# A graph network on one core: output norms, R's sums and row sums moved within a hand-written order

## The chip, the core and the metric

The kernel runs on one core of a Trainium2 chip. The metric is the device time of one execution in microseconds, the median of three: 1462.17 us before the change (1462.06 to 1468.56). The profile is one further execution with the hardware profiler on: 1480.01 us, with a span of 1478.2 us. Engines are named as in the profile: PE (TensorE, matmuls), PEld (its weight loads), DVE (VectorE), ACT (ScalarE), POOL (GpSimd), SP (SyncE, which here only issues transfers).

## What is computed

Two graph layers on 2708 nodes with 256 features, in float32. Layer 0 is `x = layernorm(x + relu([x, adj @ x] @ W + b))`. Layer 1 makes, in two steps, an attention matrix A by nucleus ("top-p") selection, and a second product with the row-normalized adjacency R:

```python
R = S + eye(N);  R = R / R.sum(-1)
for n in range(2):
    probs = softmax(q(Xa) @ k(Xa).T)          # per row: keep the largest until 0.9 of the mass
    A = probs * mask;  A = A / A.sum(-1)      # row sums
    Xf = R @ Xf
    Xa = A @ Xa
    Z = Z + Xf @ U1[n].T + Xa @ U2[n].T
h = layernorm(X + Z) * g + b                  # "middle" norm
x = layernorm(x + h)                          # "end" norm
```

The kernel applies U1 and U2 before the products, so a product of A (or R) with a projected matrix gives an output directly. adj is sparse (0.3% and the diagonal): the rows that a block of R needs are gathered.

## The kernel before, in words

Rows are treated in 22 blocks of 128 (the last has 20). All engines run the order in which the instructions are written down; there is no scheduler. Each engine works through its own queue in that order and waits at semaphores, so a waiting instruction holds back everything behind it on the same engine.

There are four stages. Layer 0 fills the first 520 us or so. The first attention step and the lists of nonzero columns come next. The third stage, the loop at L1098 over `per`, runs from about 800 us to the end; the change lies there. It does the second attention step for all blocks, both products with R, and the output norms. The fourth is a short tail.

One turn of `per` is called a block here. It has six slots, `g` = 0 to 5 (L1109), and several row blocks are in flight in it:

- Row block `per` is on DVE: `finish2` (L950) finds its threshold and makes its mask. L959 multiplies below a bound (128x2720), L962 takes maxima of 20 segments, L559 and L561 put candidates in order, L972 to L987 find the threshold, L990 marks ties, L993 writes the masked weights and, as `tot`, their sum. L994 computes the same sum in another way, as z + mass - below (`kept`), and L996 takes its reciprocal `ra`.
- Row block `per - 1` is on PE: in each slot `turn` (L520) transposes four 128x128 pieces (L526), ACT copies them from PSUM (L529), and `products` (L535, L546) multiplies the pieces of the slot before with `ya`.
- Row blocks `per + 1` and `per + 2` are on ACT: trial levels (`try_act`, L905 and L908, 128x2708 each) and exponentials of logits (`exps2`, L801 and L805).
- R's product is cut into units of one matmul each (`r_units`, L701, L713), eight to a row block. Blocks 0 to 9 do the product of step 0, blocks 11 to 21 that of step 1 at 16 units each: 2, 3, 3, 2, 3, 3 by slot, so a row block of R begins in slots 0 and 3 and ends in slots 2 and 5. When one begins, its successor's rows are fetched into the other half of `yg` by seven indirect gathers that POOL issues (`y_load`, L677, L681), and its adjacency by SP (L687).
- A sum of R that has ended is taken by DVE one slot later: the list `later` holds it. `r_out` (L733) is L736 in step 0; in step 1 it calls `arrive` (L744, L751), which adds the part to a base kept in memory (`za_d`). The attention's part arrives likewise, in slot 1.
- When both parts have arrived, a row block is `ready`. `final_slot` (L1054) takes up to two of them in slot 3. In slot 4 it takes statistics of them and of the ones in their second norm (L1021, L1022, on DVE) and the root of the variances (L1064, on ACT). In slot 5 it does the reciprocal and a product (L1066, L1067, on DVE), the norms (L1031, on ACT), the store of finished blocks (L1052, issued by SP), and for new ones the scale and the addition on POOL (L1046, L1047).

`bulk` keeps figures per row block for one check at the end (`flags`); where a flag is set, another, general path computes everything anew. With this data it is not taken.

Of the kernel before, what the change touches and what calls it, by code (L numbers as in the profile page):

```python
# [9 lines left out]
FP = mybir.dt.float32  # L10
# [10 lines left out]
P = 128  # L21
# [7 lines left out]
WS = 5  # L29
# [119 lines left out]
def fast_path(ctx, tc, c, flags, fint, xT_d, x_d, w0_d, b0_d, w1_d, w2_d, w3_d, u1_d, u2_d, g_d, b_d):  # L149
# [521 lines left out]
    r_now = []  # L671
    r_in, a_in, y_in = {}, {}, {}
    arrived, loads, held = {}, {}, {}
    later = []
    ready = []

    def y_load(s, m):  # L677
# [23 lines left out]
    def r_units(n):  # L701
        for _ in range(n):
            s, m = r_queue[0]
            p = rows(m)
            if not r_now:
                r_now[:] = [ps_misc(), 0]
                if m + 1 < NB:
                    r_load(s, m + 1)
            acc, k = r_now
            a, y = r_in[s, m]  # L710
            kw = CW if k < CC else p
            rhs = v[:p, m, :] if s and k == CC else y[:kw, k, :]
            nc.tensor.matmul(acc[:p, :D], lhsT=a[:kw, k, :p], rhs=rhs, start=k == 0, stop=k == CC)  # L713
            r_now[1] += 1
            if k == CC:
                r_now.clear()
                r_queue.pop(0)
                r_in.pop((s, m))
                base = za_load(m) if s else None
                later.append(lambda s=s, m=m, acc=acc, base=base: r_out(s, m, acc, base))  # L720

    def za_load(m):

# [52 lines left out]

    bulk = small.tile([P, 4 + WS, NB], FP, tag="bulk", name="bulk", bufs=1)
    nc.gpsimd.memset(bulk[:, :3, :], 1.0)  # L780
    nc.gpsimd.memset(bulk[:, 3:, :], 0.0)

    class Block:

# [165 lines left out]
    def finish2(b):  # L950

        t, p = b.t, b.p
        sc = small.tile([P, 3 + 2 * WS], FP, tag="sc", name="sc", bufs=3)
        below, mass, nk = (sc[:p, i:i + 1] for i in range(3))
        num, run = bulk[:p, 4:, t], sc[:p, 3:3 + WS]
        need, kept, tot = (bulk[:p, i, t:t + 1] for i in range(1, 4))
        th = b.m
        e = e2(t)[:p]
        nc.vector.scalar_tensor_tensor(w[:p], e, b.d, e, op0=ALU.is_lt, op1=ALU.mult, accum_out=below)  # L959
        cand = small.tile([P, NS2 * 8], FP, tag="cand", name="cand", bufs=2)  # L960
        for i in range(NS2):
# [25 lines left out]
        nc.vector.tensor_scalar(part[:p], part[:p], th, None, op0=ALU.mult)  # L987
        W = NW // WS
        for i in range(WS):
            nc.vector.match_replace(w[:p, W * i:W * (i + 1)], part[:p, i, :], e[:, W * i:W * (i + 1)], 3.0e38)  # L990
            if i == WS // 2:
                yield
        nc.vector.scalar_tensor_tensor(e, w[:p], th, e, op0=ALU.is_gt, op1=ALU.mult, accum_out=tot)  # L993
        nc.vector.scalar_tensor_tensor(kept, mass, below, b.z, op0=ALU.subtract, op1=ALU.add)  # L994
        ra = small.tile([P, 1], FP, tag="ra", name="ra")
        nc.vector.reciprocal(ra[:p], kept)  # L996
        ras[t] = ra

    new, finals = [], []
    tail = []  # L1000

    mvs = small.tile([P, 4, 2], FP, tag="mvs", name="mvs", bufs=1)
# [4 lines left out]
    class Final:  # L1007
# [39 lines left out]
            nc.gpsimd.tensor_tensor(h[:p], h[:p], self.x1[:p], op=ALU.add)  # L1047

        def end(self):
            t, p = self.t, self.p  # L1050
            self.norm(self.h)
            nc.sync.dma_start(out=out_d[t * P:t * P + p, :], in_=self.h[:p])  # L1052

    def final_slot(i):  # L1054

        if i == 3:
            while ready and len(new) < 2:
                new.append(Final(*ready.pop(0)))
                new[-1].load()
        n = len(new) + len(finals)  # L1060
        if i == 4 and n:
            for k, f in enumerate(new + finals):
                f.stats(k)
            nc.scalar.activation(sds[:, :n], mvs[:, :n, 1], AF.Sqrt, bias=c.eps, scale=1.0)  # L1064
        if i == 5 and n:
            nc.vector.reciprocal(sds[:, :n], sds[:, :n])  # L1066
            nc.vector.scalar_tensor_tensor(nbs[:, :n], mvs[:, :n, 0], -1.0, sds[:, :n], op0=ALU.mult, op1=ALU.mult)  # L1067
            for f in finals:
                f.end()
            for f in new:  # L1070
                f.middle()
            finals[:] = new
            new.clear()

# [23 lines left out]
    for per in range(NB + 1):  # L1098
# [9 lines left out]
            b_exp = blocks[per + 2] = Block(per + 2)  # L1108
        for g in range(NG):  # L1109
            n = n_r * (g + 1) // NG - n_r * g // NG  # L1110
            now, later[:] = later[:], []
            if g == 0:
                if b_exp:
                    shift(b_exp, lg[0])
                r_units(n)
            if per:
                turn(t_mul, g, ya, accs[t_mul], e2(t_mul))
            if b_exp and g == 3:
                lg = logits(1, b_exp.t, 2)
            if g == NG - 1 and 3 < per + 3 < NB:  # L1120
                lg = logits(1, per + 3, 0)
            if g:
                r_units(n)
            if b_exp and g == 1:
                lg = logits(1, b_exp.t, 1)
            products(1 if per else 0)
            if b_exp and g in (0, 1, 3):
                exps2(b_exp, (g + 1) // 2, *lg)
            if b_act:
                for k, part in {0: ((0, 0),), 1: ((0, 1), (0, 2), (0, 3)), 2: ((1, 0),), 3: ((1, 1), (1, 2), (1, 3))}.get(g, ()):  # L1130
                    try_act(b_act, k, part)
            if g == 0:
                if b_dve:
                    last_level(b_dve)
                    masks = finish2(b_dve)
                    next(masks)
                if per > 1:

                    t = t_mul - 1
                    base = za_load(t)  # L1140
                    later.append(lambda t=t, base=base: arrive(t, base, accs.pop(t), ras.pop(t)[:rows(t)]))
            elif masks:
                next(masks, None)
                if b_exp and g == 5:
                    begin_search(b_exp)
            for f in now:
                f()
            if g:
                final_slot(g)
# [2 lines left out]

    nc.vector.tensor_scalar(flags[:, 2 * NB:3 * NB], bulk[:, 0, :], 1.0e30, None, op0=ALU.is_ge)
    nc.vector.tensor_scalar(flags[:, 3 * NB:4 * NB], bulk[:, 1, :], 0.0, None, op0=ALU.is_le)
    nc.vector.scalar_tensor_tensor(flags[:, 4 * NB:5 * NB], bulk[:, 2, :], 1.0 + TIE_EPS, bulk[:, 3, :],
                                   op0=ALU.mult, op1=ALU.is_lt)
    nc.vector.tensor_reduce(flags[:, 5 * NB:6 * NB], bulk[:, 4:, :].rearrange("p w t -> p t w"), AX.X, ALU.max)
    nc.vector.tensor_scalar(flags[:, 5 * NB:6 * NB], flags[:, 5 * NB:6 * NB], 8.0, None, op0=ALU.is_ge)
    nc.vector.tensor_reduce(fcol, flags, AX.X, ALU.add)
    products(0)  # L1160
# [3 lines left out]
    nc.vector.tensor_copy(fint, pf[:1, :1])  # L1164
    t = NB - 1
    base = za_load(t)
    while later:
        later.pop(0)()
    arrive(t, base, accs.pop(t), ras.pop(t)[:rows(t)])
    while ready or finals:  # L1170
        for g in (3, 4, 5):
            final_slot(g)
    assert not r_queue and len(arrived) == NB

# [359 lines left out]
```

## Time and profile before

| What | us | Where from |
|---|---|---|
| Timed, median of three | 1462.17 | times |
| Profiled span | 1478.2 | page |
| PE busy | 1302.5 (88%) | page, part 1 |
| DVE busy | 1047.2 (71%) | page, part 1 |
| ACT busy | 750.6 (51%) | page, part 1 |
| POOL busy | 624.6 (42%) | page, part 1 |
| One gather of step 1 (L681), mean | 0.967 | page, part 5 |
| L1046, mean | 1.645 | page, part 5 |

A line of the groups has the source line, the engine and the operation, what is written from what, the shape and the count; then busy time, the mean of one in ns, and the idle time of the engine ahead of it with what ended most of it. The list of waits gives, for pairs of waiting and waited-for instructions, the time in total, how often, and the longest. A line of the windows has the stretch, its length, the busy time and number of instructions of PE, PEld, DVE, ACT and POOL, then the clock granted to PE, the busy share of the transfer engines and their GB/s. A line of the timeline has the start, the duration, the engine, the source line, the operation, and in brackets how long the engine had been idle and what released it. "remote" and "another core or an unknown queue" stand where the profile found no releaser. In the changed kernel the lines from L995 on are shifted (L1046 becomes L1045).

### The profile page before, as it was taken

Reading aid. Unit: us, or ns where it says so; the run is one execution under the profiler, and the core shown is the slowest. Engines: PE = TensorE matmul, PEld = TensorE weight load, DVE = VectorE, ACT = ScalarE, POOL = GpSimd, SP = SyncE. Lnnn points to the kernel's source line nnn. Section 1 sums busy time; section 2 is a strip of 40 time slices with the busy share of each in tenths; the row PEclk is TensorE's granted clock in tenths of the full one; section 3 lists DMA queues with packets and bytes.
Section 4 is the critical chain, followed back from the end, with each engine's and each line's share of the span. In section 5 each row is a group of like instructions: output and inputs, shape, how many; then the busy total and the mean of one; then the engine's idle time right before and its main releaser. Section 6 shows DMA issues by size and latency. Waiting matters only on the chain.

```text
span 1478.2 us, 18958 instructions
## 1 busy us (share of the span) xinstructions
PE 1302.5 (88%) x5788; PEld 907.7 (61%) x5788; DVE 1047.2 (71%) x3500; ACT 750.6 (51%) x1351; POOL 624.6 (42%) x597
## 2 busy tenths in 40 slices
PE   8999999898999999999988599999878767787776
PEld 6877787534666666666654376767545555555553
DVE  2444546849788877677514699999987777777775
ACT  1000000145455555555544387878767777777741
POOL 1000000033644416765543667677154555555551
PEclk9999999999999999999997699999989889889996
DMA  6554444312221202322322454545142333333332
GB/s 179 179 164 150 150 149 150 107 55 77 71 70 61 63 9 73 95 66 65 64 85 84 137 164 130 171 132 163 49 140 84 103 107 108 107 116 122 108 112 52
DMA packets 92830, 157.94 MB, mean 107 GB/s; under 512 B 16356, under 2 KB 65196, under 8 KB 92720
## 3 DMA queue, kind: packets, MB, share of 16 engines
q1 hardware_dynamic: 66434, 100.59, 21.3%
q0 software_dynamic: 20544, 51.17, 13.1%
q10 hardware_dynamic: 5742, 4.89, 1.1%
q8 instruction: 48, 0.79, 0.2%
q14 instruction: 62, 0.51, 0.1%
HBM read 125.33 MB, written 31.26 MB: 106 GB/s over the span
## 4 chain that ended last, share of the span: by engine, by line
PE 55%; DVE 23%; ACT 12%; another core or an unknown queue 6%; issue 3%; DMA 0%; ACTq 0%; DVEq 0%
PE acc L546 17%; PE acc L255 14%; PE lg L506 6%; PE tr L526 4%; DVE cand L962 3%; PE misc L660 3%; DVE w L990 3%; DVE e L993 3%; DVE w L959 2%; ACT w L905 2%; ACT w L908 2%; PE acc L632 2%; ACT e L801 2%; DVE spare L561 2%
## 5 line engine op out<-in xcount | busy, mean ns | idle before, releaser
L546 PE MATMUL acc<-ya,wT 128*128 128x256 f32 (+1 forms) x924 | 247.6, 410 | 54.6 <-ACT wT L529 30.8
L529 ACT COPY wT<-tr 128x512 f32<-128x512 f32 (+2 forms) x264 | 134.2, 511 | 317.4 <-PE tr L526 145.3
L546 PEld LDWEIGHTS acc<-ya,wT 128*128 128x128 f32 (+1 forms) x924 | 180.6, 203 | 114.1 <-issue 48.6
L546 PE MATMUL acc<-x,wT 128*128 128x256 f32 (+1 forms) x924 | 234.4, 393 | 8.4 <-ACT wT L529 7.4
L681 POOL DMA_INDIRECT yg<-yf_d,ix x154 | 191.7, 1245 | 104.9 <-PE misc L713 46.1
L546 PEld LDWEIGHTS acc<-x,wT 128*128 128x128 f32 (+1 forms) x924 | 167.1, 192 | 90.9 <-issue 49.0
L713 PE MATMUL misc<-yg,adj_t 128*128 128x256 f32 (+1 forms) x660 | 181.7, 402 | 32.2 <-issue 20.4
L255 PE MATMUL acc<-y,adj_t 128*128 128x257 f32 (+1 forms) x924 | 208.8, 382 | 0.0
L365 POOL DMA_INDIRECT adj_t<-in_adj,ix x154 | 172.5, 1120 | 50.6 <-issue 39.6
L255 PEld LDWEIGHTS acc<-y,adj_t 128*128 128x128 f32 (+1 forms) x924 | 171.5, 189 | 34.0 <-issue 10.2
L681 POOL DMA_INDIRECT yg<-v_d,ix x154 | 148.9, 967 | 83.7 <-issue 40.4
L506 PE MATMUL lg<-k,q 64*128 64x512 f32 (+3 forms) x528 | 154.1, 611 | 25.4 <-ACT e L805 23.0
L526 PE MATMUL tr<-ident,e 128*128 128x128 f32 (+1 forms) x968 | 152.6, 277 | 22.7 <-issue 13.5
L713 PEld LDWEIGHTS misc<-yg,adj_t 128*128 128x128 f32 (+1 forms) x660 | 118.0, 193 | 85.3 <-issue 47.5
L526 PEld LDWEIGHTS tr<-ident,e 128*128 128x128 f32 (+1 forms) x968 | 117.3, 142 | 69.3 <-issue 42.5
L332 POOL DMA_DIRECT2D part_d<-e x1 | 0.6, 576 | 295.5 <-DVE e L331 295.5
L552 DVE MAX8 cand<-e 128x8 f32<-128x170 f32 (+1 forms) x352 | 88.2, 319 | 39.6 <-ACT e L513 23.0
L905 ACT ACTIVATE w<-e,st 128x2708 f32<-128x2708 f32 (+1 forms) x43 | 113.5, 2640 | 0.0
L908 ACT ACTIVATE w<-e,st 128x2708 f32<-128x2708 f32 (+1 forms) x42 | 111.0, 2642 | 0.1
L438 ACT COPY x1T<-tr 128x256 f32<-128x256 f32 (+1 forms) x22 | 8.0, 364 | 192.2 <-PE tr L437 192.2
L962 DVE MAX8 cand<-w 128x8 f32<-128x136 f32 (+1 forms) x440 | 94.4, 284 | 0.8
L1046 POOL TENSOR_TENSOR yg<-yg,gb 128x256 f32<-128x256 f32 x21 | 34.5, 1645 | 136.5 <-ACT yg L1031 136.5
(226 smaller groups left out, 1871.1 us busy)
## 6 DMA issues: line engine op xcount, KB each, us to landing
adj_t<-in_adj SPq DMA_DIRECT2D x44, 704.0 KB
adj_t<-adjc_d SPq DMA_DIRECT2D x44, 448.0 KB
adjc_d<-adj_t SPq DMA_DIRECT2D x22, 256.0 KB
base<-za_d SPq DMA_DIRECT2D x41, 128.0 KB
adjc_d<-adj_t SPq DMA_DIRECT2D x22, 192.0 KB
xt<-in_x ACTq DMA_DIRECT2D x21, 128.0 KB
x_d<-x SPq DMA_DIRECT2D x21, 128.0 KB
x1b_d<-xb SPq DMA_DIRECT2D x21, 128.0 KB
```

The source lines that it names most:

```text
L255: nc.tensor.matmul(acc[:p, :n], lhsT=halves[k // KH][:kw, k % KH, :p], rhs=y[:kw, k, :n], start=k == 0, stop=stop and k == NB - 1)
L365: nc.gpsimd.indirect_dma_start(out=a[:CW, i, :], out_offset=None, in_=adj_rows, in_offset=bass.IndirectOffsetOnAxis(ap=ix[:CW, m, i:i + 1] ...
L506: nc.tensor.matmul(lg[:p, h, :b - a], lhsT=q[o, t * P:t * P + p], rhs=keys[s][o, i, :b - a], start=True, stop=True)
L526: nc.tensor.transpose(tr[:kw, k % 4, :p], e[:p, k * P:k * P + kw], ident[:p, :p])
L529: nc.scalar.copy(wT[:, :full, :p], tr[:, :full, :p])
L546: nc.tensor.matmul(acc[:p, :D], lhsT=wT[:kw, k % 4, :p], rhs=y[:kw, k, :], start=k == 0, stop=k == NB - 1)
L552: nc.vector.max(dst[:p, i * 8:(i + 1) * 8], src[:p, i * step:i * step + w])
L681: nc.gpsimd.indirect_dma_start(out=y[:CW, i, :], out_offset=None, in_=rows_d, in_offset=bass.IndirectOffsetOnAxis(ap=ix[:CW, m, i:i + 1], ...
L713: nc.tensor.matmul(acc[:p, :D], lhsT=a[:kw, k, :p], rhs=rhs, start=k == 0, stop=k == CC)
L905: nc.scalar.activation(scr[:b.p, :N], e, AF.Relu, bias=b.nz, scale=b.l[k], accum_out=b.relu)
L908: nc.scalar.activation(scr[:b.p, :N], e, AF.Sign, bias=b.nz, scale=b.l[k], accum_out=b.sign)
L962: nc.vector.max(cand[:p, 8 * i:8 * i + 8], w[:p, SEG2 * i:SEG2 * (i + 1)])
```

## The change

It changes where in the order some instructions stand, and it takes one sum from another place:

- In `final_slot`, new blocks are taken in slot 2 and statistics made in slot 3. The root stands in slot 5, two slots behind its statistics. The reciprocal and the norms stand in slot 0 of the next block, behind `finish2`'s first part; the stores stand in slot 1, by the list `done`.
- `later` becomes two lists. A sum of R goes into the second one and is taken two slots behind its end; the attention's part still goes one slot on.
- The row sum `tot`, which L993 makes while it masks, is inverted directly. `below` and `mass` move into `bulk`, and the other form of the sum, which only the check needs, is formed once for all blocks at the end.

The purpose is to have an instruction wait for a result only when that result has had time to be made.

```diff
-    later = []
+    later = [[], []]
@@ r_units
-                later.append(lambda s=s, m=m, acc=acc, base=base: r_out(s, m, acc, base))
+                later[1].append(lambda s=s, m=m, acc=acc, base=base: r_out(s, m, acc, base))
@@ finish2
-        below, mass, nk = (sc[:p, i:i + 1] for i in range(3))
-        num, run = bulk[:p, 4:, t], sc[:p, 3:3 + WS]
-        need, kept, tot = (bulk[:p, i, t:t + 1] for i in range(1, 4))
+        num, run = bulk[:p, 5:, t], sc[:p, :WS]
+        need, below, mass, tot = (bulk[:p, i, t:t + 1] for i in range(1, 5))
+        nk = sc[:p, WS:WS + 1]
...
         nc.vector.scalar_tensor_tensor(e, w[:p], th, e, op0=ALU.is_gt, op1=ALU.mult, accum_out=tot)
-        nc.vector.scalar_tensor_tensor(kept, mass, below, b.z, op0=ALU.subtract, op1=ALU.add)
         ra = small.tile([P, 1], FP, tag="ra", name="ra")
-        nc.vector.reciprocal(ra[:p], kept)
+        nc.vector.reciprocal(ra[:p], tot)
@@ Final
         def end(self):
+            self.norm(self.h)
+
+        def store(self):
             t, p = self.t, self.p
-            self.norm(self.h)
             nc.sync.dma_start(out=out_d[t * P:t * P + p, :], in_=self.h[:p])
@@ final_slot
-        if i == 3:
+        if i == 2:
             while ready and len(new) < 2:
                 new.append(Final(*ready.pop(0)))
                 new[-1].load()
+        if i == 1:
+            while done:
+                done.pop().store()
         n = len(new) + len(finals)
-        if i == 4 and n:
+        if i == 3:
             for k, f in enumerate(new + finals):
                 f.stats(k)
+        if i == 5 and n:
             nc.scalar.activation(sds[:, :n], mvs[:, :n, 1], AF.Sqrt, bias=c.eps, scale=1.0)
-        if i == 5 and n:
+        if i == 0 and n:
             nc.vector.reciprocal(sds[:, :n], sds[:, :n])
...
             for f in finals:
                 f.end()
             for f in new:
                 f.middle()
+            done[:] = finals
@@ the loop over per and g
-            now, later[:] = later[:], []
+            now = later.pop(0)
+            later.append([])
...
                     next(masks)
+                final_slot(0)
                 if per > 1:
...
-                    later.append(lambda t=t, base=base: arrive(...))
+                    later[0].append(lambda t=t, base=base: arrive(...))
@@ the tail
+    kept = bulk[:, 3, :]
+    nc.vector.tensor_tensor(kept, kept, bulk[:, 2, :], op=ALU.subtract)
+    nc.vector.tensor_tensor(kept, kept, bulk[:, 0, :], op=ALU.add)
...
-    while later:
-        later.pop(0)()
+    for f in later[0] + later[1]:
+        f()
+    final_slot(0)
+    final_slot(1)
     arrive(t, base, accs.pop(t), ras.pop(t)[:rows(t)])
     while ready or finals:
-        for g in (3, 4, 5):
+        for g in (2, 3, 5, 0, 1):
             final_slot(g)
```

More of the change, by code (lines that the diff above doesn't have):

```diff
@@ L775, in fast_path @@
     nc.gpsimd.iota(ranks, pattern=[[1, 8]], base=0, channel_multiplier=0, allow_small_or_imprecise_dtypes=True)
-    bulk = small.tile([P, 4 + WS, NB], FP, tag="bulk", name="bulk", bufs=1)
-    nc.gpsimd.memset(bulk[:, :3, :], 1.0)
-    nc.gpsimd.memset(bulk[:, 3:, :], 0.0)
+    bulk = small.tile([P, 5 + WS, NB], FP, tag="bulk", name="bulk", bufs=1)
+    nc.gpsimd.memset(bulk[:, :4, :], 1.0)
+    nc.gpsimd.memset(bulk[:, 4:, :], 0.0)
     class Block:
@@ L993, in finish2 @@
         nc.vector.scalar_tensor_tensor(e, w[:p], th, e, op0=ALU.is_gt, op1=ALU.mult, accum_out=tot)
-        nc.vector.scalar_tensor_tensor(kept, mass, below, b.z, op0=ALU.subtract, op1=ALU.add)
         ra = small.tile([P, 1], FP, tag="ra", name="ra")
-        nc.vector.reciprocal(ra[:p], kept)
+        nc.vector.reciprocal(ra[:p], tot)
         ras[t] = ra
-    new, finals = [], []
+    new, finals, done = [], [], []
     tail = []
@@ L1140, in fast_path @@
                     base = za_load(t)
-                    later.append(lambda t=t, base=base: arrive(t, base, accs.pop(t), ras.pop(t)[:rows(t)]))
+                    later[0].append(lambda t=t, base=base: arrive(t, base, accs.pop(t), ras.pop(t)[:rows(t)]))
             elif masks:
@@ L1154, in fast_path @@
     nc.vector.tensor_scalar(flags[:, 3 * NB:4 * NB], bulk[:, 1, :], 0.0, None, op0=ALU.is_le)
-    nc.vector.scalar_tensor_tensor(flags[:, 4 * NB:5 * NB], bulk[:, 2, :], 1.0 + TIE_EPS, bulk[:, 3, :],
+    kept = bulk[:, 3, :]
+    nc.vector.tensor_tensor(kept, kept, bulk[:, 2, :], op=ALU.subtract)
+    nc.vector.tensor_tensor(kept, kept, bulk[:, 0, :], op=ALU.add)
+    nc.vector.scalar_tensor_tensor(flags[:, 4 * NB:5 * NB], kept, 1.0 + TIE_EPS, bulk[:, 4, :],
                                    op0=ALU.mult, op1=ALU.is_lt)
-    nc.vector.tensor_reduce(flags[:, 5 * NB:6 * NB], bulk[:, 4:, :].rearrange("p w t -> p t w"), AX.X, ALU.max)
+    nc.vector.tensor_reduce(flags[:, 5 * NB:6 * NB], bulk[:, 5:, :].rearrange("p w t -> p t w"), AX.X, ALU.max)
     nc.vector.tensor_scalar(flags[:, 5 * NB:6 * NB], flags[:, 5 * NB:6 * NB], 8.0, None, op0=ALU.is_ge)
```

## The prediction

> **What bounds the kernel now.** I read the page's busy line first: PE 88% is no bound by itself, because the clock stays near full and the engine idles in one stage only. So I took the idle times of the costliest groups (part 5 of the page), then the list of waits of the last stage, then a table of windows by block, and last the timeline of one block. Below, "slot" is one of the six turns g of a block in the last loop (L1098, L1109).
>
> First the waits of 1180 to 1400 us, six blocks of the second half of that loop (us in total, times, longest):
>
> ```profile
> POOL yg L1046 <- ACT yg L1031: 84.8, 7, 12.3
> ACT wT L529 <- remote: 53.6, 6, 9.7
> ...
> PE acc L546 <- ACT wT L529: 30.7, 7, 8.8
> ...
> DVE sds L1066 <- ACT sds L1064: 13.1, 7, 3.3
> ```
>
> POOL stands 12.1 us per block before L1046; ACT stands 8.9 us per block before one copy of turned weights, for a releaser that the trace doesn't name, and PE waits for that copy; DVE stands 1.9 us per block for the square root. Then the windows from one L993 to the next (length; busy PE, PEld, DVE, ACT, POOL):
>
> ```profile
> 1285.84:1320.95 35.11, 27.72 (x111) 18.89 (x111) 26.05 (x91) 25.04 (x41) 18.70 (x18) 0.84 0.37 113
> ...
> 1426.29:1451.53 25.24, 21.52 (x90) 15.07 (x89) 24.13 (x84) 5.16 (x11) 11.75 (x11) 0.84 0.37 83
> 960.27:984.82 24.55, 23.23 (x112) 17.13 (x111) 23.54 (x80) 20.03 (x33) 17.53 (x14) 1.00 0.51 151
> ```
>
> A block of the first half (third line) is bound by DVE: 23.5 of 24.6 us. A block of the second half (first line) has 26.1 us of DVE work and lasts 35.1, so 9 us are idle on all engines. The last block (second line), with 7 gathers instead of 14, lasts 25.2. The nine blocks from 1112.41 to 1426.29 take 313.9 us, 34.9 each.
>
> Where the 9 us lie, from the timeline:
>
> ```profile
> 1229.17 0.99 POOL L681 DMA_INDIRECT yg<-v_d,ix  x1
> ...
> 1244.18 0.18 DVE L1022 BATCH_NORM_AGGREGATE mvs<-bst 128x2 f32<-128x6 f32 x1 [1.82 <-remote]
> ...
> 1245.52 0.95 POOL L681 DMA_INDIRECT yg<-v_d,ix  x1 [0.31 <-issue]
> ...
> 1246.28 0.38 PE L713 MATMUL misc<-yg,adj_t 128*128 128x256 f32 x1 [1.74 <-issue]
> ...
> 1249.15 0.59 ACT L529 COPY wT<-tr 128x512 f32<-128x512 f32 x1 [8.79 <-remote]
> ```
>
> Here 14 gathers (L681) run back to back, one per 1.255 us, from 1229.17. From about 1240.4, 11 us in, DVE, PE and ACT stop obeying their waits promptly, though what they wait for is long done (the transpose for ACT's copy ended at 1236.3); they are free 2.7 us after the last gather was issued. The same happens once where no norm exists:
>
> ```profile
> 812.38 0.95 POOL L681 DMA_INDIRECT yg<-yf_d,ix  x1 [0.30 <-issue]
> ...
> 837.43 0.95 POOL L681 DMA_INDIRECT yg<-yf_d,ix  x1 [0.30 <-issue]
> ...
> 838.65 3.05 DVE L993 SCALAR_TENSOR_TENSOR e<-w,st,e 128x2720 f32<-128x2720 f32 x1 [7.09 <-remote]
> ...
> 842.92 0.59 ACT L529 COPY wT<-tr 128x512 f32<-128x512 f32 x1 [22.69 <-remote]
> ...
> 965.72 3.69 POOL L681 DMA_INDIRECT yg<-yf_d,ix  x1 [0.31 <-issue]
> ```
>
> An unbroken run of 21 gathers from 812.38 slows DVE from 822.9 (10.5 us in) until the run ends. In the blocks of the first half, as many gathers per block do no harm: there they come in runs of at most 8, parted by pauses of 1.6 to 2.1 us and by two stretched ones (last line) under L959 and L993. My reading: **an unbroken run of more than about 8 gathers freezes the other engines' waits until it ends.** The cause inside the chip I can't see.
>
> **What the Trainium skill says.** "SBUF — State Buffer", section "Who interferes with whom": a DVE instruction that holds the port pair shared with GpSimd blocks it completely, descriptor writing included. The trace agrees for L959 and L993: a gather beside them takes up to 3.7 us instead of 0.95, an L1046 3.19 instead of 0.73. "Perfetto Trace Analysis", section on the SWDGE timeline: the profiled end of a gather is when its descriptors are written, not when data land; the trace's queue shows packets some 2 us past the last issue. "ScalarE: Activation LUTs", section "What ACT_TABLE_LOAD costs": about 1283 ns; the trace has 1283 ns at L1064. Square root and exponential stay apart in the new order, so both loads per block remain. No page that I read names the freeze.
>
> **The change part by part.**
> *Root and norms.* Before: statistics and root in slot 4, reciprocal and norms (L1031) in slot 5, so at the block's end DVE waits for the root (1.9 us) and ACT does four norms (4 x 0.59 = 2.3 us) ahead of the next block's first copy. After: statistics in slot 3, root in slot 5, reciprocal and norms in slot 0 of the next block, behind DVE's L959 and ACT's first L905. The root is then issued over 4 us before DVE asks for it: 1.9 us fall away. No work is saved.
> *What is queued behind the norms.* On POOL, L1046 and L1047 wait for the norms. POOL's order stays 14 gathers, then four additions and products (TT below), but the seven gathers issued in slot 0 now stand before the TTs, not behind. Take s as the start of L959. Before: L1046 starts at s+0.45, falls under L959 (3.19 us), gathers start at s+6.1 (1223.09 to 1229.17). After: ACT does copy, table load, exponentials and L905 in 7.2 us from 0.7 us after L993's end, which is s-2.1; so s+5.8. Two end norms and one middle norm, 1.8 us, put the first TT at s+7.6; four TTs at 0.8 take 3.2, now under MAX8 instructions, which left them at 0.73 (1227.50). Gathers start at s+11.
> *When the run is broken.* From L959 to L993 nominally takes 20.5 us in the last block (1431.01 to 1451.53), and one more statistics pair (0.6) makes s+21.1. So 10 us, 8 gathers, run before L993 holds POOL for some 2.7 us; 2 us later L959 holds it again; then 3 or 4 gathers remain. Before, the freeze began 10 to 12 us into the run, ahead of L993, which it delayed. After, the run is cut just before that point. It is close, and it decides the result.
> *POOL's load:* 14 x 1.255 + 3.2 + 2 x 2.7 = 26.2 us per block, just under the other engines.
> *R's sums one slot later (L736, L751):* same instructions. The accumulator (two buffers) is held one slot longer; the next user comes four slots after the end, so PE waits only at the loop's start, where the first two sums leave one slot later: some 3 us more than the 3.9 us that PE waited for L736 at 812.44, hidden, since PE then stands 13.5 us for L993 anyway. The last v_d store is some 4 us later; its gathers start near 1075 instead of 1070.6 and are needed at 1086: hidden.
> *Stores in slot 1, norms in slot 0:* SP, which stood up to 25 us at L1052, gets free earlier; but for one wait of 3.3 us in all, nothing waited for it.
> *Row sum:* L994 goes (22 x 0.22 us busy), but the reciprocal now waits for L993's accumulator; starts move from 0.25 to about 0.1 us after it: 0.13 us per block, 3 us over 22. The three small flag instructions at the end cost under 1 us, beside PE.
> *Sum.* New block: DVE 26.05 - 0.2 = 25.85 us; divided by the 0.96 (23.5/24.6) that DVE reaches in the first half, 26.9. Nine blocks save 9 x (34.9 - 26.9) = 72 us, the first half 10 x 0.13 = 1, together 73 in the profiled run of 1480. Timed runs are 18 us faster (1462); if all of that lay in the freezes, the gain would be 55, if none, 73. I take 68: **1394 us**.
>
> **The rivals.**
> *Frozen in part.* The freeze begins an instant before L993, or the pause of 2.7 us isn't enough: 2 to 5 us per block remain. For it: onset at 8 to 9.5 gathers against my 8. Blocks of 30 us: 9 x 4.9 = 44, 1417 us.
> *Frozen as before.* The 14 gathers are still neighbours in POOL's order, and the freeze merely moves. Then only the root's wait goes: 9 x 1.9 = 17, 1445 us. Against it: L993 and L959 now fall into the run.
> *Slower.* With the run starting 5 us later, its end, frozen, comes after the next block's start; PE needs those rows in slots 0 and 3 and waits about 5 us per block: +45 - 17 = 28, 1490 us. For it: every gather is behind four TTs that now wait for ACT's L905. Against it: the first seven have 13 us from their start until slot 0.
>
> **How the numbers follow.** My forecast (blocks of 26.3 to 28.5 us, 1380 to 1405) has 0.62; frozen in part 0.18; frozen as before 0.13; slower 0.07. The time is that of the first. The range reaches from 1376, just below every block at DVE's bare 25.9 us (9 x 9.0 = 81 us, 1380), to 1436, where the second case ends (2 us less per block than now, and the root's). Faster by over 0.5%: the first two, and most of the third, 0.89; same 0.04; slower 0.07.
>
> **What would show it.** Right: L993 to L993 near 27 us from 1112 on; ACT's wait "remote" before L529 gone or under 2 us; the L1046 wait below 3 us per block; stretched gathers under L993 and L959 in every block. The freeze near 812 stays, which the change doesn't touch. Wrong: blocks above 29 us with that ACT wait still of 5 us or more, or PE waiting for gathers in slots 0 or 3; also a DVE wait at the new reciprocal, or at L751 for ACT's late norms.

## The result, and the profile after

The changed kernel takes 1401.85 us (1398.12 to 1404.79) where the kernel before, run beside it, takes 1463.99 us: a ratio of 0.957, with a 95% interval of 0.9536 to 0.9604. The forecast was 1394, its range 1376 to 1436. In the profiled runs the gap is larger, 1480.01 against 1402.21 us; the 1402.21 is one of the changed kernel's timed runs, the 1480.01 lies above all timed runs of the kernel before beside it (1462.06 to 1468.56). Further down it turns out that this gain belongs to the chip as much as to the kernel: on two chips the kernel before itself takes 1378 us, and variants of both kernels run within 0.3% of it.

First the list of waits of 1180 to 1360 us in the changed kernel (us in total, times, longest), beside the one shown before:

```profile
ACT wT L529 <- PE tr L526: 18.6, 7, 6.3
...
POOL yg L1045 <- ACT yg L1030: 12.8, 5, 6.6
...
PE acc L546 <- ACT wT L529: 3.8, 6, 1.3
```

ACT's wait before L529 whose releaser was "remote" (53.6 us) is gone; in all blocks but the long one shown below, ACT now waits for a transpose that PE does only then. POOL's wait for the norms falls from 12 us per block to 1.4 to 1.7 (6.6 in one block). DVE's wait for the root isn't in the list at all.

Then the windows from one L993 to the next (length; busy PE, PEld, DVE, ACT, POOL with counts; granted clock, transfer share, GB/s): a usual block of the second half and its one long block.

```profile
1264.72:1291.49 26.77, 23.91 (x112) 17.08 (x111) 25.59 (x89) 24.98 (x41) 21.00 (x19) 1.00 0.48 147
1181.78:1211.18 29.40, 23.04 (x100) 16.75 (x99) 25.70 (x89) 22.90 (x38) 19.18 (x17) 0.88 0.40 126
```

The usual block lasts 26.8 us instead of 35.1, with DVE busy for 25.6 of them: DVE bounds the block now, as it does in the first half. The time in which all engines were idle is gone, although hardly any work was removed: DVE's busy time per block has fallen by 0.5 us only.

How the gathers lie now, from POOL's timeline of a usual block:

```profile
1237.65 0.95 POOL L681 DMA_INDIRECT yg<-v_d,ix  x1 [0.30 <-issue]
1238.90 2.92 POOL L681 DMA_INDIRECT yg<-v_d,ix  x1 [0.30 <-issue]
...
1243.37 3.58 POOL L681 DMA_INDIRECT yg<-v_d,ix  x1 [0.30 <-issue]
...
1253.56 0.73 POOL L1045 TENSOR_TENSOR yg<-yg,gb 128x256 f32<-128x256 f32 x1 [1.61 <-ACT yg L1030]
...
1256.74 0.99 POOL L681 DMA_INDIRECT yg<-v_d,ix  x1
```

The gather at 1237.65 is the seventh of its run. The next falls under L993 (from 1237.95) and takes 2.92 us, the one at 1243.37 falls under L959 and takes 3.58, four more follow, and then POOL waits 1.6 us for the norms. So the run is cut before the freeze, as foreseen. The Trainium skill, "SBUF — State Buffer", section "Who interferes with whom", says that a DVE instruction with two inputs in SBUF contends with a GpSimd instruction that reads SBUF. L993 and L959 have two such inputs, and a gather takes its list of rows (`ix`) from SBUF. The trace agrees: beside them a gather takes 2.92 and 3.58 us instead of 0.95. Here this does the kernel good.

One block is a trial that the kernel makes by itself. There the run had started earlier, and nine undisturbed gathers start ahead of L993 instead of seven (timeline of all engines, changed kernel):

```profile
1171.61 0.99 POOL L681 DMA_INDIRECT yg<-v_d,ix  x1
...
1181.78 3.05 DVE L993 SCALAR_TENSOR_TENSOR e<-w,st,e 128x2720 f32<-128x2720 f32 x1
...
1187.38 0.27 ACT L529 COPY wT<-tr 128x128 f32<-128x128 f32 x1 [4.43 <-PE tr L526]
1188.12 0.29 DVE L798 TENSOR_REDUCE nmax<-lg 128x1 f32<-128x128 f32 x1 [2.52 <-remote]
```

DVE stands 2.5 us for logits that PE had finished 4 us before that wait began, and the block lasts 29.4 us. Of ACT's 4.4 us only the last 1.1 are of this kind: its transposes end at 1186.30. Both waits lie behind L993, so the one stretched gather (2.75 us) didn't end the matter.

Nine gathers do not always freeze something. In the block before this one (from 1133.20, 26.9 us) nine are followed by 2.1 us without a gather. In three blocks of e12 below, nine are followed by 0.75 to 2.2 us without one, and the blocks last 26.8 to 27.1 us. In e1, nine run straight into L993 in two blocks: one lasts 26.95 us, the other 30.40. So the edge is not sharp.

### The profile page after: what moved, and what is told of

It reads as the page before. It is cut to its first block, busy times and chain, and to the rows that moved or that the text cites. A ratio compares the mean times of both kernels' runs of the same rounds, so it can differ in the third digit from the quotient of the medians.

```text
span 1400.4 us, 18930 instructions
## 1 busy us (share of the span) xinstructions
PE 1283.5 (92%) x5788; PEld 897.8 (64%) x5788; DVE 1044.5 (75%) x3482; ACT 744.5 (53%) x1345; POOL 642.3 (46%) x595
## 4 chain that ended last, share of the span: by engine, by line
PE 52%; DVE 41%; issue 3%; ACT 2%; another core or an unknown queue 1%; DMA 0%; SPq 0%; ACTq 0%; DVEq 0%
PE acc L546 15%; PE acc L255 15%; DVE cand L962 6%; DVE w L990 6%; PE lg L506 5%; DVE e L993 5%; DVE w L959 5%; PE tr L526 4%; DVE srt L559 3%; DVE spare L561 3%; PE misc L660 3%; PE acc L632 2%; PE misc L427 2%; PE acc L461 2%; PE misc L390 2%
## 5 line engine op out<-in xcount | busy, mean ns | idle before, releaser
L529 ACT COPY wT<-tr 128x512 f32<-128x512 f32 (+2 forms) x264 | 133.5, 512 | 255.5 <-PE tr L526 197.8
L546 PE MATMUL acc<-ya,wT 128*128 128x256 f32 (+1 forms) x924 | 235.0, 394 | 13.0 <-ACT wT L529 7.2
L681 POOL DMA_INDIRECT yg<-v_d,ix x154 | 195.3, 1268 | 85.5 <-PE tr L526 35.2
L546 PEld LDWEIGHTS acc<-ya,wT 128*128 128x128 f32 (+1 forms) x924 | 171.1, 193 | 68.5 <-issue 26.6
L365 POOL DMA_INDIRECT adj_t<-in_adj,ix x154 | 169.0, 1097 | 50.5 <-issue 39.5
L713 PE MATMUL misc<-yg,adj_t 128*128 128x256 f32 (+1 forms) x660 | 174.8, 399 | 14.6 <-issue 7.5
L506 PE MATMUL lg<-k,q 64*128 64x512 f32 (+3 forms) x528 | 153.3, 603 | 26.2 <-ACT e L805 24.1
L713 PEld LDWEIGHTS misc<-yg,adj_t 128*128 128x128 f32 (+1 forms) x660 | 118.9, 194 | 61.3 <-issue 28.2
L559 DVE MAX8 srt<-spare 128x8 f32<-128x128 f32 (+3 forms) x264 | 81.3, 308 | 9.1
```

Of the source, the lines that this page charges most:

```text
L365: nc.gpsimd.indirect_dma_start(out=a[:CW, i, :], out_offset=None, in_=adj_rows, in_offset=bass.IndirectOffsetOnAxis(ap=ix[:CW, m, i:i + 1] ...
L506: nc.tensor.matmul(lg[:p, h, :b - a], lhsT=q[o, t * P:t * P + p], rhs=keys[s][o, i, :b - a], start=True, stop=True)
L529: nc.scalar.copy(wT[:, :full, :p], tr[:, :full, :p])
L546: nc.tensor.matmul(acc[:p, :D], lhsT=wT[:kw, k % 4, :p], rhs=y[:kw, k, :], start=k == 0, stop=k == NB - 1)
L559: nc.vector.max(dst[:p, i:i + 8], src[:p])
L681: nc.gpsimd.indirect_dma_start(out=y[:CW, i, :], out_offset=None, in_=rows_d, in_offset=bass.IndirectOffsetOnAxis(ap=ix[:CW, m, i:i + 1], ...
```

## The experiments

Two theories stood at the outset. **A**: the gain comes from cutting the run of gathers, whose second part froze the other engines' waits. **B**: the gain comes from the waits that the new order removes by itself, DVE's for the root and ACT's norms ahead of the next block's first copy. **C**, beside them: the other two parts of the change. Lengths of blocks without a further word are means of eight blocks of the second half, from one start of L959 to the next; before it is 34.84 us, after 27.18.

The runs came in five groups, each on a chip of its own, with the kernel before beside them. Which chip the first comparison had, and which the profile of the kernel before, isn't known. That turned out to matter:

| Group | Kernels | The kernel before there, us |
|---|---|---|
| first comparison | before, after | 1463.99 |
| 1 | e1 to e4 | 1475.00 |
| 2 | e5 to e8 | 1378.07 |
| 3 | e9 | 1378.05 |
| 4 | e10 | 1465.35 |
| 5 | e11, e12 | 1476.68 |

**e1: the new slots alone.** Only new blocks to slot 2, statistics to slot 3, root to slot 5, reciprocal and norms to slot 0 of the next block, stores to slot 1:

```diff
-        if i == 4 and n:
+        if i == 3:
             for k, f in enumerate(new + finals):
                 f.stats(k)
+        if i == 5 and n:
             nc.scalar.activation(sds[:, :n], mvs[:, :n, 1], AF.Sqrt, bias=c.eps, scale=1.0)
-        if i == 5 and n:
+        if i == 0 and n:
             nc.vector.reciprocal(sds[:, :n], sds[:, :n])
```

> The kernel before with the new slots of statistics, root, norms and stores alone; R's sums and the row sums as before. Theory A (the run of 14 gathers is cut by L993, so the freeze doesn't come): nearly the whole gain, 1400 to 1408 us, and L993 to L993 near 27 us in the second half of the loop. Theory B (the waits for root and norms were the cost): the same time, but gathers may then still run 14 in a row. Theory C (R's sums or row sums matter): 1430 us or more.

Measured: 1414.74 us, ratio 0.9608 (0.9588 to 0.9628), blocks of 27.45 us. The slots bring nearly all of it. The time is 7 us above the expected range, but so is the whole chip: before takes 11 us more there than in the first comparison. The same holds for the expected ranges of e2 to e4, so with these only the ratios to before count.

**e2: R's sums a slot later, alone.**

```diff
-    later = []
+    later = [[], []]
...
-            now, later[:] = later[:], []
+            now = later.pop(0)
+            later.append([])
```

> The kernel before with only R's sums and their adding-up taken a slot later. A and B: 1460 to 1466 us, no difference. C: 1440 or less.

Measured: 1464.16 us, ratio 0.993 (0.9913 to 0.9946). Both A and B expected no difference, and 11 us were gained. The timelines tell where. At the change from step 0 to step 1, R's first 14 gathers of step 1 run in a row. In the kernel before:

```profile
1070.59 0.95 POOL L681 DMA_INDIRECT yg<-v_d,ix  x1 [31.11 <-DMA v_d<-v]
...
1086.31 3.05 DVE L993 SCALAR_TENSOR_TENSOR e<-w,st,e 128x2720 f32<-128x2720 f32 x1 [3.33 <-remote]
```

and in e2:

```profile
1066.49 0.95 POOL L681 DMA_INDIRECT yg<-v_d,ix  x1 [32.97 <-DMA v_d<-v]
...
1078.65 3.05 DVE L993 SCALAR_TENSOR_TENSOR e<-w,st,e 128x2720 f32<-128x2720 f32 x1 [1.34 <-DVE w L990]
```

The later sums make the run begin later against DVE's work, so that L993 cuts it 12 us in, and not 16 us in after having been frozen itself for 3.3 us. Two blocks that were 28.1 and 27.7 us become 25.7 and 26.2, and the row of 35 us blocks begins one block later (25.97 us where before has 33.73). On e2's own chip, e3, which leaves R's sums where they were, has 28.2, 27.0 and 32.9 us for these three. So this part did act, but through the run of gathers, not through what it was written for.

**e3: the row sum alone.** `ra` is the reciprocal of L993's own sum, and L994 goes.

```diff
-        nc.vector.scalar_tensor_tensor(kept, mass, below, b.z, op0=ALU.subtract, op1=ALU.add)
-        nc.vector.reciprocal(ra[:p], kept)
+        nc.vector.reciprocal(ra[:p], tot)
```

> The kernel before with only the row sum taken from the mask instruction itself (one small DVE instruction less per block). A and B: 0.13 us per block, 1 to 3 us in all, 1459 to 1463 us. C: 1440 or less.

Measured: 1474.35 us, ratio 0.9996 (0.9982 to 1.001), blocks of 34.80 us. The times can't tell it from nothing. The traces of this chip show it: the nine whole blocks of the first half behind the loop's first last 24.41 us on average in e3, 24.52 in e1 and 24.54 in e4, so 0.11 to 0.13 us less, about the 0.13 of the prediction.

**e4: only POOL's products moved.** Statistics, root and norms stay in slots 4 and 5; POOL's product and addition go behind the next block's gathers of slot 0.

```diff
             h = self.h
+            held_tts.append(self)
+        def tts(self):
+            p, h = self.p, self.h
             nc.gpsimd.tensor_tensor(h[:p], h[:p], c.gb[:p, 0, :], op=ALU.mult)
...
                     next(masks)
+                while held_tts:
+                    held_tts.pop(0).tts()
```

> The kernel before, statistics, root and norms (ACT, DVE) where they were; only POOL's product and addition of each middle norm (L1046, L1047) go behind the next block's seven gathers of slot 0. So POOL stands no longer 12 us for the norms, and DVE's wait for the root and ACT's norms ahead of the next copy stay. A: if the new place parts the gathers into runs of 7, most of the gain: blocks of 27 to 29 us, 1400 to 1425 us; if the trace shows runs of 10 or more that no long DVE instruction cuts, the freeze stays and 1440 or more. B: 1455 us or more whatever the runs of gathers look like.

Measured: 1412.99 us, ratio 0.958 (0.9564 to 0.9597), blocks of 27.65 us: as much as all the new slots bring, from an edit that leaves DVE, ACT and PE with their order. Waits of 1180 to 1360 us in e4:

```profile
POOL yg L681 <- PE misc L713: 18.0, 17, 2.5
...
ACT yg L1031 <- DVE nbs L1071: 16.1, 6, 3.6
...
POOL yg L1050 <- ACT yg L1031: 3.4, 4, 0.9
```

POOL no longer stands 12 us for norms, so it isn't late, and now the gathers wait for PE to free their buffer (first line): 2 us of rest after seven of them. B fails here. ACT still has its four norms ahead of the next copy, and even waits 2.7 us per block for DVE ahead of them (second line); and DVE's wait for the root, which B counted at 1.9 us, is absent from this list although root and reciprocal were not moved: that wait was a consequence of the freeze too.

**e5 to e8, on a chip where the kernel before takes 1378 us.** e5 adds work to the kernel before, six small products on POOL into an unused tile ahead of the gathers of slot 3 (2.8 us):

```diff
     def y_load(s, m):
         y = yg[:, m % 2]
+        if s and m > 1 and m % 2 == 0:
+            for _ in range(6):
+                nc.gpsimd.tensor_tensor(idle, c.gb[:, 0, :P], c.gb[:, 0, :P], op=ALU.mult)
```

> The kernel before with work added and nothing removed: six small products on POOL into a spare tile (some 2.5 us in all) ahead of the seven gathers of slot 3, in the second half of the loop. Theory A (a long unbroken run of gathers freezes the other engines): runs of 7, blocks of 27 to 30 us in place of 35 (POOL's own load is then about 29), so 1410 to 1435 us. Theory B (the waits for root and norms were the cost): these are all still there, so 1460 us or more.

Measured: 1378.45 us, ratio 1.0007 (0.9994 to 1.0021). e6 is the changed kernel with the norms put earlier in slot 0:

```diff
+            if g == 0:
+                final_slot(0)
             if b_act:
...
-                final_slot(0)
                 if per > 1:
```

> The changed kernel with the reciprocal and the norms of slot 0 put ahead of DVE's L959 and of ACT's first L905, so that POOL's products start some 7 us earlier. A: the products fall under L959 and the gathers then run for 12 to 14 us before L993 cuts them: the freeze comes back in part or whole, blocks of 29 to 35 us, 1415 to 1465 us. B: no wait for the root comes back, so as the changed kernel, 1397 to 1408 us.

Measured: 1375.69 us, ratio 0.9989 (0.9976 to 1.0001). e7 is the changed kernel with root and norms one slot earlier each and POOL's products where e4 has them:

```diff
-        if i == 5 and n:
+        if i == 4 and n:
             nc.scalar.activation(sds[:, :n], mvs[:, :n, 1], AF.Sqrt, bias=c.eps, scale=1.0)
-        if i == 0 and n:
+        if i == 5 and n:
             nc.vector.reciprocal(sds[:, :n], sds[:, :n])
...
-                final_slot(0)
+                while held_tts:
+                    held_tts.pop(0).tts()
```

> The changed kernel with the root in slot 4, reciprocal and norms in slot 5, and POOL's products behind the seven gathers of slot 0, as in the run with the products alone moved. A: POOL falls behind no more, the gathers run by sevens, parted by products or idle time, and the one frozen block goes: blocks of 26.3 to 27 us, 1392 to 1402 us. B: the order of POOL doesn't matter and the norms stand ahead of the next block's first copy again, 2.3 us per block: 1415 us or more.

Measured: 1371.19 us, ratio 0.9976 (0.9954 to 0.9999). e8 is the changed kernel with three pauses, two of them at the loop's start:

```diff
+        if (s, m) in ((0, 4), (0, 5), (1, 2)):
+            for _ in range(6):
+                nc.gpsimd.tensor_tensor(idle, c.gb[:, 0, :P], c.gb[:, 0, :P], op=ALU.mult)
```

> The changed kernel with the pause of six small products on POOL ahead of three sets of seven gathers: two at the loop's start, where 19 gathers ran in a row and DVE stood 6.6 us, and one early in the second half, where 10 ran in a row. A: the wait of 6.6 us ahead of DVE's mask in the loop's first block goes to under 2, and the run is 4 to 8 us faster than the changed kernel (ratio to before about 0.953). B says nothing of it: as the changed kernel, or 1 to 2 us slower for the added work.

Measured: 1376.1 us, ratio 0.9995 (0.998 to 1.0011). None of the four tells A from B as was planned, because on this chip there is next to nothing to gain: only e7 is faster than the kernel before, by 0.24%. Two things they do show. e6 and e8 have all the slots of the changed kernel; if the waits that B names cost the time by themselves, these two would be faster here too, and they can't be told from the kernel before. And the freeze isn't a property of the instructions alone. In e6 the run of gathers is 12 long, 14 us, before a DVE instruction cuts it (timeline of all engines):

```profile
1170.68 0.99 POOL L681 DMA_INDIRECT yg<-v_d,ix  x1
...
1184.07 0.73 ACT L529 COPY wT<-tr 128x512 f32<-128x512 f32 x2
...
1184.61 3.05 DVE L993 SCALAR_TENSOR_TENSOR e<-w,st,e 128x2720 f32<-128x2720 f32 x1
```

At 13 and 14 us into the run ACT and DVE go on without any wait. The gathers are written at the same 1.25 us each as on the other chips.

**e9 and e10: one kernel, two chips.** The kernel before with pauses of different length in six blocks of the second half, none in the others:

```diff
+    pauses = {6: (0, 6), 10: (0, 1), 12: (0, 2), 14: (0, 3), 16: (3, 6), 17: (4, 6)}
...
         for i in range(CC):
+            for _ in range(times if i == at_i else 0):
+                nc.gpsimd.tensor_tensor(idle, c.gb[:, 0, :P], c.gb[:, 0, :P], op=ALU.mult)
```

> The kernel before with pauses of different length (small products on POOL, 0.47 us each) put into the 14-gather run of some of the second half's blocks and none into others: after gather 7, six products, one, two and three; after gather 10, six; after gather 4, six; the rest without. Theory A (an unbroken run of over 8 gathers freezes the other engines, on chips where that happens at all: the last four kernels ran on a chip where the kernel before itself takes 1378 us): where the kernel before takes 1460 us or more, the blocks with six products after gather 7 last 27 to 30 us, those with none 35, those with one to three between, longer the shorter the pause; six after gather 4 leave a run of 10 and 1 to 4 us of freeze, six after gather 10 come too late, 31 us or more. In all 1430 to 1455 us. Where the kernel before takes about 1378 us, all blocks last 26 to 29 us and no dose shows. Theory B (the waits for root and norms were the cost): no dose matters on either chip.

Measured: 1377.49 us, ratio 0.9999 (0.9984 to 1.0014): again a chip without the freeze. Windows of e9, one per block from a start of L959 to the next (in this kernel's own numbering L965; columns as above), the first without a pause, the second with 0.94 us after the seventh gather:

```profile
1139.02:1166.28 27.26, 23.93 (x109) 17.64 (x108) 25.99 (x90) 24.83 (x41) 21.30 (x19) 0.94 0.51 155
...
1193.71:1220.68 26.97, 24.18 (x110) 17.81 (x110) 25.79 (x91) 24.83 (x41) 21.70 (x20) 0.94 0.46 142
```

No dose shows. The same kernel on a third chip:

> The same kernel as in the run before this one (pauses of 2.8, 0.4, 0.9, 1.4 us after gather 7, of 2.8 us after gather 10 and after gather 4, in six blocks of the second half), sent again in the hope of a chip on which the kernel before takes 1460 us or more. There, theory A: about 35 us for blocks without a pause, 27 to 30 with 2.8 us after gather 7, between them with the shorter ones; in all 1430 to 1455 us. Theory B: every block about 35 us, no difference in all. If the kernel before takes about 1378 us here too: 27.3 us for every block, and nothing told apart.

Measured: 1435.3 us, ratio 0.9799 (0.9756 to 0.9842), on a chip where the kernel before takes 1465.35. The same view of e10; pauses in order: 2.8 us after gather 7, none, 0.41, 0.94 and 1.40 us after gather 7, 2.8 after gather 10, 2.8 after gather 4:

```profile
1142.85:1170.33 27.48, 25.77 (x127) 18.99 (x126) 26.30 (x90) 24.46 (x40) 22.82 (x24) 1.00 0.42 129
1170.33:1205.30 34.97, 25.65 (x91) 17.49 (x90) 26.02 (x90) 24.96 (x41) 19.07 (x19) 0.80 0.40 121
1205.30:1240.34 35.04, 26.45 (x113) 18.90 (x112) 25.92 (x91) 25.08 (x41) 19.16 (x19) 0.90 0.37 113
1240.34:1269.31 28.97, 25.76 (x121) 18.83 (x120) 25.91 (x91) 25.17 (x41) 21.72 (x20) 1.00 0.45 137
1269.31:1296.65 27.34, 24.97 (x121) 18.18 (x121) 26.16 (x90) 24.95 (x41) 22.09 (x21) 1.00 0.45 140
1296.65:1326.07 29.42, 24.83 (x103) 17.65 (x102) 25.94 (x90) 24.94 (x41) 22.93 (x24) 0.88 0.47 139
1326.07:1352.82 26.75, 24.41 (x113) 18.28 (x112) 25.57 (x90) 24.67 (x41) 22.02 (x22) 0.94 0.44 134
```

This is the clearest result of the study. DVE is busy for about 26 us in every block; the length is 35.0 without a pause or with 0.41 us after gather 7, 29.0 with 0.94 there, and 27.3 to 27.5 with 1.40 or more there. Added work, 1.40 us of it, takes 7.6 us off a block, with the order that B blames left in place. And the block that lasts 34.97 us here without a pause lasts 27.26 on the chip of e9: the freeze costs 7.7 us per block on one chip and nothing on another.

Two other explanations fail on these traces. The granted clock is lower in the long blocks (0.80 and 0.90 in the two of 35 us), but PE is busy there for 25.7 and 26.5 us, against 24.4 to 25.8 in the five others, so PE too stands idle for most of the difference. And late data is not the cause: a pause makes the rest of the gathers later still, and the blocks get shorter. What an unpaused block of e10 looks like from inside:

```profile
1176.41 0.99 POOL L687 DMA_INDIRECT yg<-v_d,ix  x1
...
1192.74 0.94 POOL L687 DMA_INDIRECT yg<-v_d,ix  x1 [0.30 <-issue]
...
1196.23 0.59 ACT L529 COPY wT<-tr 128x512 f32<-128x512 f32 x1 [9.54 <-remote]
```

Two doses went better than expected: a pause after gather 10 was to be too late (31 us or more) and gave 29.4; a pause after gather 4 was to leave 1 to 4 us of freeze and left none, since the mask instruction (L993, here L999) cut the run six gathers after the pause.

**e11: order of e7 and short pauses; e12: the changed kernel again.** e11 has two small products (0.9 us) ahead of nearly every set of seven gathers in the first half of the loop, and ahead of slot 0's sets in the second:

```diff
+        if (m % 2 if s else m > 2):
+            for _ in range(2):
+                nc.gpsimd.tensor_tensor(idle, c.gb[:, 0, :P], c.gb[:, 0, :P], op=ALU.mult)
```

> The order of the run with norms in slot 5 and POOL's products behind the gathers of slot 0, and besides a pause of two small products (0.94 us, the shortest that kept a block under 29 us) ahead of the sets of seven gathers: in the first half of the loop ahead of nearly each, in the second ahead of those of slot 0. On a chip where the kernel before takes 1460 us or more, A: no run of gathers over 7, so nothing is frozen, at the loop's start neither; blocks of 26.8 to 28 us and a loop that starts without its 6 us of wait; 1385 to 1398 us, 5 to 15 us faster than the changed kernel beside it. B: no better than the changed kernel. On a chip where the kernel before takes about 1378 us: 1370 to 1378 us, no gain from the pauses.

> The changed kernel itself, on the same chip as the run beside it. A: where the kernel before takes 1460 us or more, 0.953 to 0.961 of it as measured before; where it takes about 1378 us, no freeze is there to be taken away, and the change brings what is left of its gain, 0.1 to 0.4 us per block: 1372 to 1377 us, ratio 0.996 to 1.000. B: the waits for root and norms are there on every chip, so a ratio of 0.96 on every chip.

Measured: e11 1403.79 us, ratio 0.9501 (0.9474 to 0.9529); e12 1404.6 us, ratio 0.9517 (0.949 to 0.9545); before takes 1476.68 on that chip. e12 repeats the first comparison, with a somewhat larger gain (72 us). e11 can't be told from e12, so its expectation fails. It does take the freeze from the loop's start: the loop's first whole block lasts 24.46 us, where e12 has 34.28. But it has one of 33.67 us two blocks later (timeline of all engines, e11):

```profile
859.43 0.99 POOL L686 DMA_INDIRECT yg<-yf_d,ix  x1 [0.28 <-PE misc L718]
...
867.95 0.89 POOL L683 TENSOR_TENSOR idle<-gb 128x128 f32<-128x128 f32 x2
...
879.49 0.48 DVE L741 SCALAR_TENSOR_TENSOR v<-misc,rinv,v 128x256 f32<-128x256 f32 x1 [6.39 <-remote]
```

Seven gathers, 0.9 us of rest and seven more freeze DVE for 6.4 us. In e10 0.94 us had nearly been enough, but there the mask instruction cut the run five gathers later. So the choice of the shortest dose was wrong: after such a pause, the count of gathers doesn't start anew. Whether 1.4 us does so, e10 can't tell either, as a DVE instruction cut those runs too. Of the versions run where the freeze exists (e1 to e4, e10, e11), none is shown to beat the changed kernel. e7 wasn't run there, and its timeline has runs of 12 or 13 gathers in three blocks of the second half.

## Why the prediction was right, point by point

- **The block is bound by no engine, and an unbroken run of gathers freezes the others.** Shown, by e10's doses (35.0 to 27.3 us by a pause) and by e4. (The prediction's remark that the clock stays near full does not fit its own windows, 0.84 in the second half; PE is no bound all the same, as it stands idle there.) What the prediction did not say is that this holds for some chips only: three groups of runs and the first comparison had it, two had not. The changed kernel itself was not run on the latter, only its variants e6 to e8.
- **"More than about 8" gathers, 10 to 12 us in.** Right as a rough figure: seven gathers before the cut leave blocks of 26.8 us, and with nine some blocks are frozen in part (29.4 us here, 30.4 in e1) and some are not. "Until it ends" is too simple: in the block of 29.4 us the freeze comes behind the cut.
- **Gathers start at s+11, L993 at s+21.1.** In the block with s = 1243.08 they start at 1256.74, s+13.7, and L993 follows at 1264.72, s+21.6. The mis-sized term is the start of ACT's chain. I let the first copy begin at s-1.4, 0.7 us after L993's end. It begins at s+1.8:

```profile
1241.76 1.28 ACT L1070 ACT_TABLE_LOAD   x1
...
1244.87 0.59 ACT L529 COPY wT<-tr 128x512 f32<-128x512 f32 x1 [1.52 <-PE tr L526]
...
1251.91 1.08 ACT L1030 ACTIVATE yg<-yg,nbs,sds 128x256 f32<-128x256 f32 x2
```

  ACT does the root's table load first, and then waits for the transpose, which stands behind other products on PE. The rest of the chain, 7.0 us to the norms, was sized well (7.2). The error of 2.7 us was on the safe side: seven gathers start ahead of L993 and not eight. This was luck. The last runs that start where the prediction put them, at s+11.0 to s+11.7, are one here, three in e12 and two in e1, and two of these six blocks were frozen in part.
- **DVE's wait for the root, 1.9 us per block.** It went, but it was no gain of its own: e4 and, on its chip, e9 leave root and reciprocal in their old slots, and neither shows it between 1120 and 1350 us.
- **Row sum, 0.13 us per block.** Blocks of the first half went from 24.53 to 24.47 us on average; beside e1 and e4, e3 has 0.11 to 0.13 us less. So the size holds, as far as such small differences between single traces can show it.
- **R's sums a slot later cost and bring nothing.** Wrong by itself: e2 gained 0.7%. I looked for what waits for the sums and found it hidden, and didn't ask what the shift does to the phase between the run of gathers and L993, though the whole forecast rested on that phase. How much of this remains beside the new slots, no run isolates: e1 and e12 ran on different chips.
- **Blocks of 26.9 us, nine of them saving 72.** From L993 at 1100.56 to that at 1344.84 they last 244.3 us, 27.1 each, the frozen one included; without it 26.9. Nine times (34.9 - 27.1) is 70.
- **1394 us.** The timed gain was 62 us, the profiled one 78. I set 55 to 73 by asking how much of the profiled run's excess of 18 us lay in the freezes, and took 68. That question was badly put. In the changed kernel and in all twelve experiments the profiled run is one of the timed runs, so profiling adds nothing that shows; the 1480.01 of the kernel before is as much as it takes on the chips of groups 1 and 5 (1470 to 1483), and may simply come from such a chip. The 8 us by which the forecast is low are within that unknown. On e12's chip the gain is 72 us, as much as the blocks' sum. The upper end of the range, 1436, doesn't follow from its own words either: 2 us less per block and the root's 1.9 make 9 x 3.9 = 35 us, so 1427.
- **The freeze at the loop's start stays.** It did: 6.6 us before L993 at 831.35 in the changed kernel. On the chips without the freeze the loop's first whole block lasts 24 us, here 32.6, and the kernel before 35.2.
- **The rivals.** Frozen in part was true of one block in nine. Frozen as before did not come. The slower case did not come: PE's one wait for gathers in the list is of 0.8 us.

## What to carry to other kernels

When all engines idle at the same time and the profile names no releaser, look at what a fourth engine does just then in an unbroken run, and move that run, or part it by pauses of several lengths, before believing any named wait: here the waits for norms and for the root fell away with it. Where timing rests on the phase between two engines, every edit near them acts on it, also one that costs nothing by its own count. And run the kernel before on several chips before a gain is credited to an edit: in four of six groups of runs the freeze was there to be removed, in two it was not, and there two variants of the changed kernel (e6, e8) gain nothing that can be measured.

## What the runs showed of the hardware

- Some chips freeze in long runs of indirect gathers and some don't, with the same kernel (e9, e10) and the same spacing of 1.25 us. Whether it is the chip for good or its state at the time, one group of runs on each can't tell. The kernel before takes 1464 to 1477 us on the ones and 1378 on the others, and this difference of 86 to 99 us is more than the change saves. Part of it is the second half of the loop (eight blocks of 34.84 us against 27.1 in e9, which has pauses in six of them), part the loop's first block (35.2 against 24.0), and the loop also starts 17 us earlier in e9 than in the kernel before (its L959 at 791.59 and 808.15). That last part wasn't looked into.
- A pause of 1.4 us after seven gathers, together with the mask instruction five gathers later, removed the freeze of a run of 14; one of 0.4 us did nothing. Seven gathers, 0.9 us of rest and seven more froze DVE for 6.4 us (e11).
- What in the chip causes it stays open. The waits in the kernel's code alone don't explain it, since e9 and e10 are the same program and only one of them freezes. The transfers go on during a freeze: in the kernel before, from 1241 to 1249 us, at 97 GB/s. Gathers are written at the same pace on both sorts of chips (medians 1.251 us in e9, 1.254 in e10). What differs between the chips, the profile doesn't show.
